# Third-layer attention units placed between second-layer units of later batches, in one fused four-layer kernel

## The chip, the cores and the metric

The kernel runs on one core of one Trainium2 chip. The metric is the time of one execution in device microseconds (us). Two differences matter for reading it: the time of an execution lies 1.7 us above the span that its profile covers, and the three timed executions before lie 0.15% apart.

## The reference

Four residual blocks run over x, four batches of 1024 tokens with 128 features, all float32. Each adds a layer-normed block output to x:

```
x = x + LN(attention0(LN(x)))     16 heads of 8, causal, scores clipped to +-10
x = x + LN(block1(LN(x)))         latent attention with rope, then a mixture of experts
x = x + LN(attention2(LN(x)))     16 heads of 8, causal, plain softmax
x = x + LN(low_rank_ffn(LN(x)))   128 -> 32 -> 512, gelu, 512 -> 32 -> 128
```

Batches are independent of each other. Within a batch each block needs the one before it. The latent attention has 16 heads; a head's query and key are 16 latent and 32 rope features wide, the key is the same for all heads. The experts are one shared and eight routed ones of which the two best count.

## The kernel before, in words

**Stages and units.** Three classes hold the work: `First` (attention0, L552), `Second` (block1, L675) and `Third` (attention2 and the low-rank part, L949). A stage is one class on one batch, 12 in all, numbered 0 to 11: 0 to 3 are First, 4 to 7 Second, 8 to 11 Third. A stage has four units of four heads, so there are 48 units. Before, units run in the order of their numbers: 0 to 15 First, 16 to 31 Second, 32 to 47 Third. A unit has 20 steps (`UNIT`), counted by `at`; step 20n is the start of unit n.

**The main loop** (L1341) runs over units, over two halves of 512 queries (`h`), and over tiles of keys. For each tile it records, on every engine's queue in program order:
- `scores` (L1251): TensorE multiplies keys by queries into PSUM tiles `ps_k`. Operands lie in `strips`, three buffers that units use in turn (`n % 3`). A First or Third head takes 32 rows of the TensorE array, so four heads can run side by side; a Second head takes 64 rows, so two can, and keys come from `kT`.
- `weigh` (L1265): ScalarE takes the exponential into `pt`; GpSimd masks the diagonal (L1279). For First, VectorE clips.
- `products` (L1213): TensorE multiplies `pt` by the values into `av`, a step or so later. At the end of a half ScalarE copies `av` to `num`, and `to_tokens` transposes and divides it.
- `max_step` (L1181): for Second and Third, whose softmax needs the row maximum, TensorE computes the scores of a *later* unit once more the other way round into `ps_q`, and VectorE reduces them to `mx`. `negated_rows` puts the negated maxima into a row of that unit's `strips`. `maxima` (L1328) sets the step at which each of a unit's 20 `max_step`s begins: 22 steps ahead for Second, 19 for Third, one a step.

In Third units `scores` takes one pair of heads (`pp`) at a time and the `max_step` beside it takes the other pair of the array's rows (L1359 to L1370); in First units `scores` takes both pairs at once.

**PSUM** has eight banks: in Second and Third one for `av` and a ring of seven (`ring`, L1344) for everything else, one bank of 512 columns a tile. A tile waits until the one seven tiles ahead of it has been read.

**Side work.** What stands before and after a stage's attention is cut into pieces by generators: `take_in` (norm, transposes, projections), `prepare` of each unit (fills its `strips` by DMAs; for Second also `roped`, L661: product, copy to `rb`, DMA that swaps neighbouring rows, two multiplications and an addition), and `tail` (output projection, norm, experts or low-rank part, residual). After each tile `other_work` (L1315) lets `pick` (L1285) choose pieces by due date: `ahead` (L1129) gives the steps before a unit's start in which `prepare` may begin and is due; inputs and tails have due dates at L1294 and L1249. What is not done when it is needed is finished on the spot, all its pieces one behind the other (`need_prep`, `need_input`, `need_tail`, `need_free`). A `prepare` of a unit that follows one of other layout clears its `strips` first (`clear`, L289: a memset and an addition on GpSimd).

**Queues.** The order of instructions on each engine is the program order; nothing is moved by a scheduler. DMAs go on SyncE's queue but for a few at the start.

**The last unit** (47) hands its rows in four quarters to `quarter` (L1045), which do the low-rank part of the last 1024 tokens, after what is left of the tails.

Of the kernel before, what the change touches and what calls it, by code (L numbers as in the profile page):

```python
# [16 lines left out]
P = 128  # L17
# [121 lines left out]
def sandwich(ctx: ExitStack, tc: tile.TileContext, a: dict, out: bass.AP):  # L139
# [69 lines left out]
    w3_n = stage[:, 2048 : 2048 + 3 * D]  # L209
# [5 lines left out]
    later(out=w3_n, in_=a["L1_attn_w_qkv"])  # L215
# [66 lines left out]
    w3 = ctile([P, 3, D], "w3")  # L282
# [23 lines left out]
    def prepare_weights():  # L306
# [74 lines left out]
        nc.gpsimd.tensor_copy(w3.rearrange("p s e -> p (s e)"), w3_n)  # L381

# [87 lines left out]
    def project(packed, w, xT, copy):  # L470

        yield RING, 1
        t = pool2.tile([P, T], F32, tag=f"packed{len(packed)}", name="packed")
        packed.append(t)
        by_half(copy, t, product(w, xT, "ps_p"))
# [76 lines left out]
    class First:  # L552
# [43 lines left out]
        def take_in(self):  # L596
            self.xT = new_xT("xT1")
            self.unit = {}
            if self.b == 0:
                xn = pool1.tile([P, NT, D], F32, tag="xn", name="xn")  # L600
                self.packed = [pool2.tile([P, T], F32, tag=f"packed{s}", name="packed") for s in range(2)]
                self.v, self.unit[0], self.mv = vs[0], strips[0], new_stats()
                yield from self.begin(xn, 0)
                self.second = Task(self.begin(xn, 1), 7)
                urgent.append(self.second)
                return
# [32 lines left out]
        def result(self, g, h):  # L639
            if g == 0 and h == 0:  # L640
                self.att = pool2.tile([P, NT, D], F32, tag="y", name="att1")
# [19 lines left out]
    def roped(dst, w, xT):  # L661
# [6 lines left out]
        nc.vector.tensor_tensor(dst[0:n], rb[0:n], cos[0:n], ALU.mult)  # L668
        for c in range(2):
            yield LIGHT, 2 * (1 - c)  # L670
            cols = slice(512 * c, 512 * c + 512)
            nc.gpsimd.tensor_tensor(swapped[0:n, cols], swapped[0:n, cols], sin[0:n, cols], ALU.mult)  # L672
            nc.gpsimd.tensor_tensor(dst[0:n, cols], dst[0:n, cols], swapped[0:n, cols], ALU.add)

    class Second:  # L675
# [41 lines left out]
        def prepare(self, g, n):  # L717
            if g == 0:
# [3 lines left out]
                self.kT = pool2.tile([P, T], F32, tag="packed0", name="kT2")  # L722
# [3 lines left out]
                rp = pool2.tile([P, T], F32, tag="packed1", name="rpk")  # L726
                yield from roped(rp, wkr.rearrange("p j r -> p (j r)"), self.xT)
                yield LIGHT, 2
                for j in range(2):
                    nc.sync.dma_start(out=self.kT[64 * j + 32 : 64 * j + 64], in_=rp[32 * j : 32 * j + 32])  # L730
            if g % 2 == 0:
# [4 lines left out]
                by_half(nc.scalar.copy, lat, product(w, self.xT, "ps_l"))  # L736
            yield RING, 1
            rp = pool2.tile([P, T], F32, tag="packed1", name="rp")
            yield from roped(rp, w2r[:, 4 * g : 4 * g + 4].rearrange("p h r -> p (h r)"), self.xT)
            yield LIGHT, 2  # L740
            while step_now[0] < strips_free(n):
                yield LIGHT, 1
            t = self.unit[g] = strips[n % 3]
            nc.sync.dma_start(
                out=t[R:P:64].rearrange("o s (q c) -> o (s q) c", q=NT),
                in_=no_max[0:2].unsqueeze(1).to_broadcast([2, 2 * NT, P]),
            )
            for j in range(4):
                pp, at, h = j // 2, 64 * (j % 2), 4 * (g % 2) + j
                nc.sync.dma_start(out=t[at : at + R, pp, :], in_=self.lat[R * h : R * h + R, :])  # L750
                nc.sync.dma_start(out=t[at + 32 : at + 64, pp, :], in_=rp[32 * j : 32 * j + 32, :])
# [197 lines left out]
    class Third:  # L949
# [8 lines left out]
        def take_in(self):  # L958
            self.unit = {}
            self.xT = new_xT("xT3")  # L960
# [7 lines left out]
        def prepare(self, g, n):  # L968
            yield LIGHT
            if n < 2 * B * NG + 3:  # L970
# [24 lines left out]
        def result(self, g, h):  # L995
            if g == 0 and h == 0:
                self.y = pool2.tile([P, NT, D], F32, tag="y", name="y3")
# [47 lines left out]
        def quarter(self, num, k):  # L1045
# [11 lines left out]
            if k == 1:  # L1057
                work, xb = tile("rb"), pool2.tile([P, T], F32, tag="packed0", name="xb")
# [70 lines left out]
    def ahead(u):  # L1129

        return (48, 44) if u.width == R else (40, 28) if u.has_max else (33, 8)
# [3 lines left out]
    units = [(layer[b], g) for layer in layers for b in range(B) for g in range(NG)]  # L1135
    stages = [u for layer in layers for u in layer]
    inputs = [Task(u.take_in(), u.pieces[0]) for u in stages]
    prep = [Task(u.prepare(g, n), (9, 4, 5, 4)[g] if u.width == R else 1) for n, (u, g) in enumerate(units)]
    tails = [None] * len(stages)
# [3 lines left out]

    def need_tail(k):

        while tails[k] is None or not tails[k].done:
            behind.popleft()[1].finish()

    def need_free(k):

        while not stages[k].att_free:
            behind[0][1].look(step_now[0])
            behind[0][1].piece(step_now[0])
            if behind[0][1].done:
                behind.popleft()

    def need_prep(n):
        for i in range(n + 1):
            if not prep[i].done:
                need_input(i // NG)  # L1160
                prep[i].finish()

    def need_input(k):
        for i in range(k + 1):
# [4 lines left out]

    def max_tiles(n):  # L1170

        mx, beside = {}, units[n][0].width != R
        for h in range(2):
            tiles = max_parts_of(h)
            if h and not beside:
                tiles = [tiles[i] for i in (0, 4, 1, 5, 2, 6, 3)]
            for i, parts in enumerate(tiles):
                for pp in (1, 0) if beside else (0, 1):
                    yield n, h, parts, pp, mx, i == len(tiles) - 1 and pp == 1 - beside

    def max_step(n, h, parts, pp, mx, last):  # L1181
# [4 lines left out]
        ps = rtile("ps_q")  # L1186
        for qt, c, at, w in parts:
            for jj in range(2):
                q, k = u.rows(g, pp, jj)
                nc.tensor.matmul(  # L1190
                    ps[jj][:, at : at + w], lhsT=q[:, qt * P : (qt + 1) * P], rhs=k[:, 512 * c : 512 * c + w],
                    start=True, stop=True,
                )
        for jj in range(2):
            for qt, c, at, w in parts:
                scores, to = ps[jj][:, at : at + w], mx[h][:, qt - 4 * h, pp, jj, c : c + 1]
                if c == h:

                    nc.vector.tensor_tensor_reduce(
                        scores, scores, cmask[:, 512 - w : 512], 1.0, -3.0e38, ALU.add, ALU.max, to  # L1200
                    )
                else:
                    nc.vector.tensor_reduce(to, scores, AX.X, ALU.max)
# [9 lines left out]
    def products(n, h, parts, first, last, state, pts):  # L1213
# [11 lines left out]
        if last:  # L1225
# [14 lines left out]
            k = n // NG  # L1240
            if g == 0 and h == 0 and k > 0:
                if u.width == R or stages[k - 1].width == R:
                    need_free(k - 1)
                elif k > 1:
                    need_free(k - 2)
            urgent.append(Task(back()))
            if g == NG - 1 and h == 1:
                tails[k] = Task(after(urgent[-1], u.tail()), u.pieces[1])
                behind.append((UNIT * NG * (k + 2) - 5, tails[k]))  # L1249
# [35 lines left out]
    def pick(at, taken):  # L1285
# [10 lines left out]
        if i is not None and inputs[i // NG].done and at >= UNIT * i - ahead(units[i][0])[0]:  # L1296
            found.append((UNIT * i - ahead(units[i][0])[1], prep[i]))
        k = next((k for k, t in enumerate(inputs) if not t.done), None)
        if k is not None and at >= UNIT * NG * (k - 1) and (k < B or tails[k - B] and tails[k - B].done):
            found.append((UNIT * NG * k - ahead(stages[k])[0], inputs[k]))  # L1300
        while behind and behind[0][1].done:
            behind.popleft()
# [24 lines left out]

    maxima = deque(  # L1328
# [101 lines left out]
```

## Time and profile before

| | |
|---|---|
| median of three executions | 2202.6 us (2199.86 to 2203.24) |
| profiled execution: time, span | 2196.13 us, 2194.4 us |
| TensorE matmul busy | 2062.8 us, 94% |
| VectorE busy | 1457.2 us, 66% |
| ScalarE busy | 1251.0 us, 57% |
| GpSimd busy | 589.5 us, 27% |
| mean granted TensorE clock | 0.97 |
| DMA | 20 GB/s, 42.93 MB |

The profile is of one execution. Busy TensorE time is the union of modelled matmul spans, and says nothing of how much of the array they fill: two heads on half of the rows count as much as four on all. Tiles go by the program's names; nearly all instructions have one line, L113, that of the recording helper. A unit's end is read from the trace as the start of the ScalarE copy `num<-av` of its second half.

### The profile page before, as it was taken

The page shows a single profiled execution, that of the slowest core. Times are in us where ns is not written, and L with a number is a line of the kernel's source. Part 1 is how long each engine was busy: PE and PEld are TensorE (multiplying, and loading weights), DVE is VectorE, ACT ScalarE, POOL GpSimd, SP SyncE. Part 2 cuts the span into 40 slices and gives each one's busy share as a digit, 9 for nine tenths or more (in the row PEclk, how much of TensorE's full clock was granted, in tenths as well). Part 3 has the DMA queues.
Part 4 walks back from the last instruction along what each step waited for, and adds up shares of the span by engine and source line. Part 5 has one row for each costly group of instructions (what it writes and reads, how often), then busy time and mean ns, then how long its engine had stood idle before and what let it go on. Part 6 is the DMA issues. An engine that isn't in the chain of part 4 may idle for free.

```text
span 2194.4 us, 40088 instructions
## 1 busy us (share of the span) xinstructions
PE 2062.8 (94%) x14480; PEld 939.4 (43%) x14480; DVE 1457.2 (66%) x4201; ACT 1251.0 (57%) x2360; POOL 589.5 (27%) x840
## 2 busy tenths in 40 slices
PE   7999999789999999999999999899999999999994
PEld 3334333334444544454444444344444444444432
DVE  4677776477666675567556675368778678777755
ACT  4777778524554554355534544255556766766775
POOL 3343333223232211222122311121113233323332
PEclk9999999989999999999999999899999999999996
DMA  2310000011111100111011100000000000000000
GB/s 59 69 17 11 12 11 11 21 38 25 28 42 26 25 16 22 35 29 26 6 30 35 29 13 1 11 7 7 6 7 7 12 7 16 8 11 17 7 1 20
DMA packets 32245, 42.93 MB, mean 20 GB/s; under 512 B 11552, under 2 KB 23840, under 8 KB 32048
## 3 DMA queue, kind: packets, MB, share of 16 engines
q1 hardware_dynamic: 31440, 40.04, 8.3%
q8 instruction: 115, 1.88, 0.3%
q14 instruction: 82, 0.67, 0.1%
q10 hardware_dynamic: 608, 0.33, 0.1%
HBM read 5.74 MB, written 2.10 MB: 4 GB/s over the span
## 4 chain that ended last, share of the span: by engine, by line
PE 82%; DVE 7%; ACT 5%; POOL 3%; issue 2%; DMA 1%; SPq 0%; ACTq 0%; POOLq 0%; DVEq 0%
PE ps_k L113 29%; PE ps_q L113 17%; PE av L113 17%; PE pgu L113 3%; ACT pt L113 2%; PE ps_a L113 2%; PE py L113 2%; DVE ps_q L113 2%; PE pa L113 2%; PE ps_p L113 1%; PE ps_o L113 1%; PE ps_t L113 1%; DVE mx L113 1%; DVE pt L113 1%; PE ps_l L113 1%
## 5 line engine op out<-in xcount | busy, mean ns | idle before, releaser
L113 ACT ACTIVATE pt<-ps_k 128x512 f32<-128x512 f32 (+2 forms) x1600 | 916.7, 631 | 621.4 <-PE ps_k L113 449.5
L1279 POOL TENSOR_SCALAR_AFFINE_SELECT pt<-pt 128x256 f32<-128x256 f32 (+1 forms) x576 | 302.8, 535 | 1209.4 <-ACT pt L113 887.4
L113 DVE CUSTOM_DVE_ANT_0 ps_q<-ps_q,cmask 128x512 f32<-128x512 f32 (+3 forms) x1024 | 488.4, 512 | 208.1 <-PE ps_q L113 187.6
L113 PE MATMUL ps_k<-strips 32*128 32x512 f32 (+3 forms) x3072 | 541.1, 527 | 9.8 <-DVE mx L113 4.9
L113 DVE TENSOR_REDUCE mx<-ps_q 128x1 f32<-128x512 f32 x512 | 328.3, 684 | 169.9 <-PE ps_q L113 168.5
L113 PE MATMUL ps_q<-strips 32*128 32x512 f32 (+3 forms) x1536 | 393.1, 530 | 14.1 <-DMA strips<-no_max 10.6
L113 PE MATMUL ps_q<-kT,strips 64*128 64x512 f32 (+3 forms) x1536 | 312.8, 491 | 25.1 <-DMA strips<-rp 24.2
L113 PE MATMUL av<-pt,vals 128*32 128x512 f32 (+3 forms) x3072 | 321.0, 500 | 15.7 <-POOL pt L1279 9.1
L113 PEld LDWEIGHTS ps_k<-strips 32*128 32x128 f32 x3072 | 220.2, 185 | 253.6 <-issue 76.3
L113 PE MATMUL ps_k<-strips,kT 64*128 64x512 f32 (+3 forms) x1536 | 323.3, 508 | 2.6 <-issue 2.6
L113 DVE TENSOR_SCALAR pt<-pt 128x1024 f32<-128x1024 f32 (+1 forms) x320 | 224.6, 717 | 115.7 <-ACT pt L113 114.1
L113 PEld LDWEIGHTS ps_q<-kT,strips 64*128 64x128 f32 x1536 | 150.0, 189 | 143.7 <-issue 100.5
L113 PEld LDWEIGHTS ps_k<-strips,kT 64*128 64x128 f32 x1536 | 133.9, 187 | 146.9 <-issue 66.2
L113 PEld LDWEIGHTS ps_q<-strips 32*128 32x128 f32 x1536 | 160.5, 184 | 64.8 <-ACT pt L113 26.2
L113 PEld LDWEIGHTS av<-pt,vals 128*32 128x32 f32 x3072 | 72.1, 109 | 218.6 <-issue 121.5
L113 PE MATMUL av<-pt,v2l 128*32 128x512 f32 (+3 forms) x1536 | 159.6, 503 | 0.0
L113 DVE DVE_READ_ACCUMULATOR2_ANT mx<- 128x1 f32 x1024 | 144.5, 141 | 0.0
L401 POOL TENSOR_TENSOR rs<-rs,minus_half 128x8 f32<-128x8 f32 (+1 forms) x38 | 63.6, 1674 | 242.4 <-DVE rs L113 239.6
L113 PEld LDWEIGHTS av<-pt,v2l 128*32 128x32 f32 x1536 | 33.7, 109 | 101.1 <-issue 72.7
L113 ACT COPY num<-av 128x512 f32<-128x512 f32 (+1 forms) x98 | 56.7, 581 | 19.8 <-PE av L113 19.7
L672 POOL TENSOR_TENSOR swapped<-swapped,sin 128x512 f32<-128x512 f32 (+1 forms) x40 | 50.8, 1271 | 63.1 <-DMA swapped<-rb 63.1
L113 PEld LDWEIGHTS ps_a<-ident,num 128*128 128x128 f32 x384 | 40.7, 141 | 61.7 <-issue 42.2
(278 smaller groups left out, 1646.0 us busy)
## 6 DMA issues: line engine op xcount, KB each, us to landing
swapped<-rb SPq DMA_DIRECT2D x32, 256.0 KB
strips<-rp SPq DMA_DIRECT2D x64, 128.0 KB
strips<-packed SPq DMA_DIRECT2D x248, 32.0 KB
strips<-lat SPq DMA_DIRECT2D x64, 64.0 KB
strips<-nT SPq DMA_DIRECT2D x256, 1.0 KB
strips<-nT SPq DMA_DIRECT2D x128, 2.0 KB
x<-in_L_attn_x_dram SPq DMA_DIRECT2D x3, 512.0 KB
out_dram<-x SPq DMA_DIRECT2D x3, 512.0 KB
```

What stands on the lines that cost most here:

```text
L113: return call(*args, **kw)
L401: nc.gpsimd.tensor_tensor(rs[:, t], rs[:, t], minus_half[:, t], ALU.pow)
L672: nc.gpsimd.tensor_tensor(swapped[0:n, cols], swapped[0:n, cols], sin[0:n, cols], ALU.mult)
L1279: nc.gpsimd.affine_select(out=corner, in_=corner, compare_op=ALU.is_ge, fill=0.0, base=0, pattern=[[0, 2], [0, n], [1, P]], channel_multip ...
```

## The change

The order of units is written out. Stages 0 to 5 run as before. Then units of stage 6 (Second, batch 2) alternate with those of stage 8 (Third, batch 0), and units of stage 7 with those of stage 9, with a last (7,2), (7,3), (9,2), (9,3). Stages 10 and 11 run as before. So units 24 to 39 mix both layers. What follows from it:
- The steps of `max_step` and `scores` change where neighbours differ. A Third unit behind a Second one (`together`) has its maxima of both pairs at once, four heads and four PSUM tiles in every second step. A Third unit before a Second one (`wide`) has its scores of both pairs at once. `beside`, one pair next to the other, stays between two Third units. The lead of the maxima is 19, 20 or 22 steps (`lead`).
- Due dates come from the new order (`due_input`, `due_tail`, `may_input`); tails that have not begun are sorted by due date. `ahead` is (40, 30) for Third, before (40, 28), and (34, 20) for First, before (33, 8).
- In Second units `other_work` is called twice a tile with a limit of three light pieces, before once with four.
- Buffers: `kT` has its own tag; `packed` and the results of First and Third (`yb`) have one buffer, before two; Second's result keeps two. With one buffer, a stage's first result waits for the tail of the stage before of the same layout (`need_free`). `roped` works in place in `rb`, and sends it by a function that it is given. `w3` takes the place of `w1` and is loaded by stage 8's `take_in`, without staging and copy.

```diff
-    w3 = ctile([P, 3, D], "w3")
+    w3 = w1
...
-    def roped(dst, w, xT):
+    def roped(w, xT, send):
         n = w.shape[1]
         rb = pool1.tile([P, T], F32, tag="rb", name="rb")
         by_half(nc.scalar.copy, rb[0:n], product(w, xT, "pa"))
         for o in range(2):
             nc.sync.dma_start(out=swapped[o:n:2, :], in_=rb[1 - o : n : 2, :])
-        nc.vector.tensor_tensor(dst[0:n], rb[0:n], cos[0:n], ALU.mult)
         for c in range(2):
             yield LIGHT, 2 * (1 - c)
             cols = slice(512 * c, 512 * c + 512)
+            nc.vector.tensor_tensor(rb[0:n, cols], rb[0:n, cols], cos[0:n, cols], ALU.mult)
             nc.gpsimd.tensor_tensor(swapped[0:n, cols], swapped[0:n, cols], sin[0:n, cols], ALU.mult)
-            nc.gpsimd.tensor_tensor(dst[0:n, cols], dst[0:n, cols], swapped[0:n, cols], ALU.add)
+            nc.gpsimd.tensor_tensor(rb[0:n, cols], rb[0:n, cols], swapped[0:n, cols], ALU.add)
+        yield LIGHT, 2
+        yield from send(rb)
...
-                self.kT = pool2.tile([P, T], F32, tag="packed0", name="kT2")
+                self.kT = pool2.tile([P, T], F32, tag="kT", name="kT2")
...
+            if self.b == 0:
+                yield LIGHT
+                nc.sync.dma_start(out=w3[:, 0:3], in_=a["L1_attn_w_qkv"].rearrange("p (s e) -> p s e", s=3))
...
-            if n < 2 * B * NG + 3:
+            if units[n - 3][0].width == R:
                 clear(strips[n % 3])
...
-                self.y = pool2.tile([P, NT, D], F32, tag="y", name="y3")
+                self.y = pool1.tile([P, NT, D], F32, tag="yb", name="y3")
...
-        return (48, 44) if u.width == R else (40, 28) if u.has_max else (33, 8)
+        return (48, 44) if u.width == R else (40, 30) if u.has_max else (34, 20)
...
-    units = [(layer[b], g) for layer in layers for b in range(B) for g in range(NG)]
+    whole = lambda *ks: [(k, g) for k in ks for g in range(NG)]
+    order = whole(0, 1, 2, 3, 4, 5)
+    order += [(6, 0), (8, 0), (6, 1), (8, 1), (6, 2), (8, 2), (6, 3), (8, 3)]
+    order += [(7, 0), (9, 0), (7, 1), (9, 1), (7, 2), (7, 3), (9, 2), (9, 3)] + whole(10, 11)
+    units = [(stages[k], g) for k, g in order]
...
+    def due_input(k):
+        return UNIT * starts[k] - (48 if stages[k].has_max else 34)
+
+    def due_tail(k):
+        return min([UNIT * (ends[k] + NG) - 5] + [due_input(k + B) - 28 if k < 2 * B else UNIT * len(units) - 30])
...
+    def beside(n):
+        return units[n][0].width != R and units[n - 1][0].width != R
+
+    def together(n):
+        return n < len(units) and units[n][0].width != R and units[n - 1][0].width == R
...
-        ps = rtile("ps_q")
+        tiles = [(pp, rtile("ps_q")) for pp in pps]
...
-            if g == 0 and h == 0 and k > 0:
-                if u.width == R or stages[k - 1].width == R:
-                    need_free(k - 1)
-                elif k > 1:
-                    need_free(k - 2)
+            if g == 0 and h == 0:
+                for m in like(k)[-1:]:
+                    need_free(m)
...
+    def lead(n):
+        return 19 if beside(n) else 22 if units[n - 1][0].width == R and not together(n) else 20
...
-        (UNIT * n + i - (22 if units[n][0].width == R else 19), m)
+        (UNIT * n + i * (1 + together(n)) - lead(n), m)
...
+                wide = not u.has_max or n == len(units) - 1 or u.width != R and units[n + 1][0].width == R
+                often = u.width == R or u.has_max and wide and n < len(units) - 1
+                pts = []
+                for pps in ((0, 1),) if wide else ((0,), (1,)):
+                    pts += [weigh(n, h, parts, ps) for ps in scores(n, h, parts, pps)]
+                    if not u.has_max:
+                        next_products(1)
+                    for pp in pps:
+                        at += 1
+                        if maxima and maxima[0][0] <= at:
+                            max_step(*maxima.popleft()[1])
+                        if pp == 0 and (u.has_max and (u.width != R or together(n + 1))):
+                            next_products(0)
+                        if pp == 0 and often:
+                            other_work(at, 3)
+                if u.has_max:
+                    next_products(0)
+                other_work(at, 3 if often else 4)
```

`like(k)` lists the stages of the same layout that run before stage k; `starts` and `ends` hold the unit at which a stage begins and the one after its last.

## The prediction

> **What bounds the kernel now.** First the page:
> ```profile
> span 2194.4 us, 40088 instructions
> PE 2062.8 (94%) x14480; PEld 939.4 (43%) x14480; DVE 1457.2 (66%) x4201; ACT 1251.0 (57%) x2360; POOL 589.5 (27%) x840
> ```
> TensorE (PE) looks full, but a matmul on half of the array's rows counts as one on all. So I cut the span at units (windows; the rows shown are units 14, 15, 16 to 23, 24 to 29, 30, and 36 to 46):
> ```profile
> core 0: us, PE busy (x) PEld busy (x) DVE busy (x) ACT busy (x) POOL busy (x), PEclk, DMA share, GB/s
> ...
> 401.80:465.70 63.90, 42.73 (x264) 16.80 (x264) 29.00 (x65) 24.04 (x34) 21.60 (x24) 0.84 0.15 39
> 465.70:522.70 57.00, 52.19 (x310) 20.90 (x310) 44.86 (x128) 22.30 (x34) 17.89 (x22) 0.94 0.15 35
> 522.70:962.60 439.90, 434.90 (x2738) 207.35 (x2740) 282.73 (x855) 220.60 (x450) 108.64 (x147) 0.99 0.10 26
> 962.60:1320.90 358.30, 350.68 (x2174) 170.05 (x2176) 232.22 (x700) 179.01 (x374) 82.16 (x112) 0.99 0.10 24
> 1320.90:1400.20 79.30, 68.65 (x384) 32.18 (x386) 33.47 (x85) 28.57 (x57) 13.43 (x17) 0.89 0.05 8
> ...
> 1649.70:2117.00 467.30, 462.45 (x3510) 208.30 (x3510) 351.82 (x1145) 317.19 (x672) 148.22 (x202) 1.00 0.05 10
> ```
> Then the timeline of PE, for what its work costs when nothing waits, a Second and a Third unit:
> ```profile
> 644.13 1.13 PE L113 MATMUL ps_k<-strips,kT 64*128 64x512 f32 x4
> 645.10 1.02 PE L113 MATMUL ps_q<-kT,strips 64*128 64x512 f32 x4
> 645.95 1.02 PE L113 MATMUL ps_k<-strips,kT 64*128 64x512 f32 x4
> ...
> 1800.30 0.70 PE L113 MATMUL ps_k<-strips 32*128 32x512 f32 x2
> ...
> 1800.84 0.59 PE L113 MATMUL ps_k<-strips 32*128 32x512 f32 x2
> ```
> Read starts, not durations. Two float32 matmuls of 512 columns on 64 rows each, two passes, take 645.95 - 645.10 = 0.85, so 0.43 us a pass; the one before came behind another array shape and took 0.97. Over the whole trace a pass that ends in a change of shape is 0.09 to 0.10 longer (`av` to `av` 0.453, `av` to 32 rows 0.543, median starts). With four groups of 32 rows a pass takes 0.53.
>
> From these I add up each unit's *dense* time: its passes at 0.43 per 512 columns of the full array, 0.095 a change of shape, 0.10 more for a 512 pass in four row groups. Measured less dense:
> - units 14 and 15 (First into Second): 120.9 - 72.0 = 48.9
> - 16 to 23 (Second): 439.9 - 414.2 = 25.7, 3.2 a unit; 24 to 29: 358.3 - 329.5 = 28.8, 4.8 a unit. 17 to 19, with little side work, lie at 0.5, 1.4 and 1.4.
> - 30 to 35 (Second into Third): 328.8 - 270.0 = 58.8
> - 36 to 46 (Third): 467.3 - 360.9 = 106.4, 9.7 a unit
>
> Second is bound by PE. Third is not: VectorE (DVE) is busy 351.8 of 467.3, 75%, against 64% in Second, and holds the banks:
> ```profile
> PEld ps_k L113 <- DVE mx L113: 41.9, 65, 1.0
> ```
> (waits, units 36 to 46). The two changes of layer hold stalls of their own, each with a cold clock behind it:
> ```profile
> PE ps_q L113 <- DMA strips<-rp: 18.7, 1, 18.7
> ...
> PE ps_q L113 <- DMA strips<-no_max: 10.6, 1, 10.6
> ```
> (waits of unit 14, then of unit 30). In 14, unit 16's whole `prepare` is finished on the spot, 419.9 to 445.9 on the chain. In 30, two strips are cleared at 1.81 + 1.89 each on GpSimd (POOL), then twelve DMAs go out, and clock 0.89 follows.
>
> **The change part by part.** Work on PE, DVE and ScalarE (ACT) stays the same: both programs hold the same matmuls and maxima. What differs is who stands beside whom. I took the dense time of each unit of the changed program from its order of instructions.
>
> *First into Second.* `ahead` of First lets unit 15's `prepare` go at step 266, due at 280 instead of 292; so unit 16's begins at step 284, not at 296, and is spread up to step 298; its first `max_step` comes at 300. The chain before, first product to landed strips, took 26.0; in place in `rb`, the second rope's copies wait for the first's DMA (2.3 by the chain's rows), so 29. Sixteen steps at 1.35 (27 a unit, units 12 and 13) cover 21.6; 7 remain where 18.7 stood. Unit 14 then has dense 28.9 + 6.5 (12 and 13: 7.1 and 6.0) + 7; unit 15 dense 39.3 + 13 (17.5 before, less 6% of 57 for the clock, and a little idling). Sum 94.7 against 120.9: 26 won. Bounds: 33 without the wait, 14 if 18.7 stays and only the cold clock goes.
>
> *Units 16 to 23.* Tail 4 is due at step 424, before 475, and squeezes into units 20 to 22. Dense 420.6, with 3.2 a unit 446.3: 6 lost.
>
> *The mixed units, 24 to 37.* Dense 659.6. A mixed pair has DVE work of a Second and a Third unit: (515.0 / 14 + 351.8 / 11) / 2 = 34.4 a unit, 66% of the 51.9 a unit that come out below. That is near Second's 64%, so I take the excess of units 24 to 29, 4.8, and not Third's 9.7: 659.6 + 14 x 4.8 = 726.8. Bounds: 1.1 (units 17 to 19) and 9.7. In its favour: four heads of one unit at once need no partner, while before `ps_k` and `ps_q` shared the array only if both had banks. Against it: `together` asks for four of seven banks at once.
>
> Inside this sum stands the price of the mixing: changes of array shape in units 24 to 46 go from 577 to 862 (32-row to `av`, which shows no price, left out). 285 x 0.095 = 27 us, already in the dense times.
>
> [...]
>
> *Units 38 to 46, Third alone.* Tail 7 now falls into units 38 to 40. Dense 329.3, with 9.7 a unit 416.6. Bounds: 7 a unit, since the fullest Third unit, 34 (dense 50.4), lay only 1.8 over; 11.7, if three runs of pieces finished on the spot (below) each stall 6.
>
> Units 24 to 46 together: 726.8 + 416.6 = 1143.4, before 358.3 + 79.3 + 249.5 + 467.3 = 1154.4: 11 won, the stall of unit 30 included. That stall goes since clears now come ten or more steps before use. There are eight clears instead of three, 5 x 3.7 = 18.5 more on POOL, which is 25% busy in these units. Cover: masks (`pt`) queue behind a clear and `av` behind them; `products` come a tile later, some 4 us, as long as a clear. If that cover fails, at most 18.5.
>
> *The end.* Before, twelve pieces of tail 10 are left after the loop; its last norm stands on the chain from 2139.94 to 2146.10. Now tail 10 ends in unit 47's first steps: 6 won.
>
> *At nothing:* `w3` is one DMA of 196 KB at step 450, used some steps later, with DMA at 10 to 26 GB/s; without that cover, a DMA wait like 10.6. The cosine product in halves adds some 0.15 x 20 on DVE, hidden as DVE has a third free. SyncE's DMAs are the same but for order; the maxima's `nT` queue behind strips that wait for a free `rb`, 20 steps ahead of use. Units 0 to 13: dense 302.1 to 303.4, 1 lost.
>
> Sum: 26 - 6 + 11 + 6 - 1 = 36. The profiled execution becomes 2196.1 - 36 = 2160; the median of the runs lies 6.5 above it, so 2202.6 - 36 = 2167.
>
> **Rivals.**
> 1. *Mixed units as dense as 17 to 19*, 1.1 a unit. For: the same DVE share, PE alone binding. Against: those units had hardly any side work. 14 x 3.7 = 52 more: 2115. Chance 0.17.
> 2. *Slower: the ring of seven banks.* In a `together` step four `ps_q` are read by DVE at 0.65 each, 2.6, and the next four can't start before; PE has `av`, `ps_k` and `ps_k` between, 1.0 + 0.95 + 0.86. On diagonal tiles (0.582 and 0.300 for two parts) DVE needs over 3. Then mixed units keep Third's 9.7: 14 x 4.9 = 69, and the median is 2202.6 + 33 = 2236. It decides from 4.8 + 36 / 14 = 7.4 a unit. Against: side work fills PE meanwhile, and half of the mixed units take two banks at a time. Chance 0.17.
> 3. *Work finished on the spot.* With one `yb`, units 33, 40 and 44 need the tail before at once: the instruction order shows 7 + 20, 29 + 20 and 7 + 20 pieces (of two tails) in one place. If each run idles PE like unit 30's stall, 10.6, then 30 are lost: 2197. For: unit 14 did this. Against: most pieces are norms on DVE and ACT, and experts' products follow each other with three in flight. Chance 0.10.
> 4. *The transition keeps its stall*, the change not doing what its due dates say: 26 less, 2193. Chance 0.06.
>
> **How the numbers follow.** The forecast has 0.50, its own range 2140 to 2195. Faster by over 0.2% (about what a measurement of this kernel can tell from no change): forecast, 1 and 4 and a part of 3, 0.77; within: 0.05; slower: rival 2 and a little, 0.18. The range from 2112 to 2214 leaves out half of rival 1 and most of rival 2.
>
> **What would show it.** Right: the first `ps_q` of unit 16 waits under 10 us and unit 14 takes under 50; no wait on `strips<-no_max`; units 27, 28, 30 and 35 (dense 37 to 40) end within 45; DVE busy near 66% in the mixed units; Third units from 41 on as before. Wrong: waits of `ps_q` or `ps_k` on `DVE mx` as long in the mixed units as in Third now (rival 2), or idle PE with a clock under 0.9 in units 33, 40 or 44 (rival 3).

## The result, and the profile after

The changed kernel takes 2270.8 us (median of four executions, 2269.0 to 2276.8) where the kernel before took 2202.0 beside it: a ratio of 1.0319, with a 95% interval of 1.0301 to 1.0336. It is slower by 3%, outside the forecast's range and above rival 2's 2236 as well. The profiled execution is a typical one, 2269.19 us with a span of 2267.5.

The page after, first its span and then the busy time of each engine:

```profile
span 2267.5 us, 40162 instructions
...
PE 2098.0 (93%) x14480; PEld 909.8 (40%) x14480; DVE 1483.1 (65%) x4221; ACT 1245.2 (55%) x2360; POOL 614.0 (27%) x849
```

The same 14480 matmuls are recorded as in the trace before. PE is busy 35 us longer, and idle 38 us longer (169.5 against 131.6). The windows of the changed kernel are cut at the same units as before: unit 14, unit 15, units 16 to 23, 24 to 37 (the mixed ones), 38 to 46, and the end.

```profile
core 0: us, PE busy (x) PEld busy (x) DVE busy (x) ACT busy (x) POOL busy (x), PEclk, DMA share, GB/s
413.10:462.30 49.20, 38.94 (x242) 13.81 (x242) 31.64 (x61) 23.68 (x33) 23.70 (x23) 0.90 0.19 51
462.30:521.50 59.20, 51.85 (x318) 20.44 (x316) 45.41 (x119) 21.99 (x33) 18.87 (x22) 0.94 0.09 23
521.50:978.10 456.60, 444.15 (x2742) 206.10 (x2742) 292.78 (x867) 221.77 (x459) 117.75 (x149) 0.99 0.10 25
978.10:1751.80 773.70, 733.48 (x4776) 305.76 (x4780) 492.93 (x1504) 388.00 (x818) 187.09 (x245) 0.97 0.07 17
1751.80:2195.20 443.40, 415.63 (x3065) 190.38 (x3062) 316.85 (x1003) 263.24 (x560) 113.87 (x160) 0.97 0.04 8
2195.20:2267.50 72.30, 42.96 (x279) 18.15 (x277) 33.31 (x118) 49.75 (x124) 16.07 (x25) 0.76 0.05 15
```

Read the first number behind the window, its length, against the prediction's terms:

| units | before | forecast | after | miss |
|---|---|---|---|---|
| 0 to 13 | 401.8 | 402.8 | 413.1 | +10.3 |
| 14, 15 | 120.9 | 94.7 | 108.5 | +13.8 |
| 16 to 23 | 439.9 | 446.3 | 456.6 | +10.3 |
| 24 to 46 | 1154.4 | 1143.4 | 1217.0 | +73.6 |
| the end | 77.4 | 71.4 | 72.3 | +0.9 |

Two thirds of the miss lie in units 24 to 46. DVE there is at 64% in the mixed units (492.93 of 773.7), a little under what the forecast took, so DVE did not become the bound. The waits of PE say what did happen:

```profile
PE av L113 <- POOL pt L1331: 32.3, 26, 6.7
PE ps_q L113 <- DVE mx L113: 23.9, 10, 10.7
PE ps_ct L113 <- DVE comb L113: 12.2, 3, 6.4
...
PE ps_q L113 <- DMA strips<-rb: 7.8, 1, 7.8
PE ps_k L113 <- DVE mx L113: 7.1, 7, 4.3
PE ps_o L113 <- ACT attT L113: 6.5, 2, 5.1
```

The columns are total us, number of waits, longest. The totals are made by a few long waits of *different* kinds: a mask on POOL (`pt`), the gates of the experts (`comb`), a norm (`mx`, 10.7, see below). The waits for strips are as forecast: one of 7.8 before unit 16's first `ps_q`, none on `no_max`.

Ten stalls of 2.5 us or more stand in units 24 to 46 (24, 25, 30, 32, 33, twice in 34, 39, 40 and 44); before there were three (26, 30 and 32). All but the one of 2.6 in unit 25 have a slow clock with them. Windows of the changed kernel right behind five of the stalls of the whole trace (the clock is the third number from the end):

```profile
785.00:800.00 15.00, 12.04 (x54) 5.42 (x56) 11.48 (x44) 3.82 (x9) 0.84 (x2) 0.77 0.00 0
...
1312.00:1325.00 13.00, 12.74 (x77) 5.18 (x81) 4.85 (x15) 4.26 (x11) 2.28 (x5) 0.77 0.27 58
1508.00:1522.00 14.00, 13.57 (x64) 4.88 (x64) 10.60 (x41) 7.08 (x17) 4.18 (x3) 0.72 0.00 1
...
1892.00:1910.00 18.00, 17.35 (x88) 5.68 (x88) 11.34 (x27) 11.55 (x25) 2.78 (x3) 0.83 0.11 17
2071.00:2085.00 14.00, 13.61 (x56) 4.68 (x56) 7.92 (x21) 8.93 (x21) 2.54 (x2) 0.71 0.19 36
```

**The account used from here on.** Each time of units 24 to 46 is split into four parts: the *dense* time of the prediction (with 0.095 a change of array shape in it), the time that PE is *idle*, the *clock* (half of PE's busy time in stretches where the clock records show 0.5; in these a pass of `ps_o`, 128x128, takes 0.213 before another, elsewhere 0.112, median starts in the changed trace), and the *rest*, which is what is left: what PE's work takes beyond dense at full clock, such as half-filled arrays (a pass of `ps_k` of 512 columns in two row groups of 32 takes 0.524 before `av`, in four 0.538, again in that trace). The *excess* over dense, by which the prediction goes, is idle, clock and rest together.

| kernel | units 24 to 46 | dense | shape changes | idle | clock | rest |
|---|---|---|---|---|---|---|
| before | 1154.4 | 960.3 | 577 | 28.1 | 14.4 | 151.6 |
| changed | 1217.0 | 988.9 | 862 | 68.0 | 25.8 | 134.3 |
| difference | +62.6 | +28.6 | +285 | +39.9 | +11.4 | -17.3 |

A part of the gain that the forecast counted on is there: the rest falls by 17.3. The shape changes are in the dense time as forecast, 27 us. The 51 us more of idle time and slow clock were not forecast.

### The profile page after: what moved, and what is told of

Same layout as the page of the kernel before. It is cut to its first block, busy times and chain, and to the rows that moved or that the text cites. A ratio compares the mean times of both kernels' runs of the same rounds, so it can differ in the third digit from the quotient of the medians.

```text
span 2267.5 us, 40162 instructions
## 1 busy us (share of the span) xinstructions
PE 2098.0 (93%) x14480; PEld 909.8 (40%) x14480; DVE 1483.1 (65%) x4221; ACT 1245.2 (55%) x2360; POOL 614.0 (27%) x849
## 4 chain that ended last, share of the span: by engine, by line
PE 77%; DVE 9%; ACT 5%; POOL 4%; issue 3%; DMA 1%; SPq 0%; ACTq 0%; DVEq 0%; POOLq 0%
PE ps_k L113 26%; PE av L113 17%; PE ps_q L113 17%; PE pgu L113 3%; PE ps_a L113 2%; ACT pt L113 2%; DVE ps_q L113 2%; DVE mx L113 2%; PE py L113 2%; PE pa L113 2%; PE ps_p L113 1%; PE ps_t L113 1%; PE ps_o L113 1%; PE ps_v L113 1%; DVE pt L113 1%
## 5 line engine op out<-in xcount | busy, mean ns | idle before, releaser
L113 PE MATMUL ps_k<-strips 32*128 32x512 f32 (+3 forms) x3072 | 476.1, 531 | 11.3 <-DVE mx L113 5.9
L113 PE MATMUL av<-pt,vals 128*32 128x512 f32 (+3 forms) x3072 | 338.1, 506 | 23.1 <-POOL pt L1331 17.8
L113 PE MATMUL ps_q<-kT,strips 64*128 64x512 f32 (+3 forms) x1536 | 335.8, 507 | 19.1 <-DVE mx L113 8.5
L113 PE MATMUL ps_k<-strips,kT 64*128 64x512 f32 (+3 forms) x1536 | 339.4, 523 | 4.7 <-issue 2.1
L113 PE MATMUL ps_q<-strips 32*128 32x512 f32 (+3 forms) x1536 | 302.7, 534 | 15.9 <-DVE mx L113 15.4
L113 PEld LDWEIGHTS ps_k<-strips 32*128 32x128 f32 x3072 | 193.6, 186 | 236.3 <-issue 94.2
L113 PEld LDWEIGHTS ps_k<-strips,kT 64*128 64x128 f32 x1536 | 133.1, 188 | 166.4 <-issue 64.5
L113 PE MATMUL av<-pt,v2l 128*32 128x512 f32 (+3 forms) x1536 | 167.6, 503 | 14.5 <-POOL pt L1331 14.5
L113 PEld LDWEIGHTS av<-pt,vals 128*32 128x32 f32 x3072 | 78.6, 109 | 234.7 <-issue 123.9
L113 PEld LDWEIGHTS ps_q<-strips 32*128 32x128 f32 x1536 | 121.5, 186 | 80.9 <-DVE mx L113 29.9
L113 PE MATMUL ps_a<-ident,num 128*128 128x128 f32 x384 | 65.5, 294 | 0.0
```

What stands on the lines that cost most here:

```text
L113: return call(*args, **kw)
```

## The experiments

**1. The changed kernel with the units in the old order.** Everything else of the change is kept: buffers, due dates, `roped` in place, `w3`.

```diff
-    order = whole(0, 1, 2, 3, 4, 5)
-    order += [(6, 0), (8, 0), (6, 1), (8, 1), ...
+    order = whole(0, 1, 2, 3, 4, 5, 6, 7, 8, 9, 10, 11)
```

> The changed kernel with its units in the old order (stages 0 to 11 one after the other), all else of the change kept. Theory A (the mixing leaves the tails too few units, so their chains and the runs of pieces finished on the spot stall PE): the stalls of units 20 to 40 of the changed kernel mostly go, those of the one result buffer (three runs) stay, the first transition's and the end's gain stay: 2195 to 2220 us. Theory B (buffers and due dates are what costs, whatever the order): 2245 us or more. Theory C (the mixed units themselves are slow, rival 2 of the forecast): below 2200, as nothing mixed is left.

Measured: 2212.4 us, ratio to before 1.006 (1.0041 to 1.0079), within theory A's range. So the mixing itself costs 58 us, and the rest of the change 12. Against this run, units 24 to 46 of the changed kernel are 53.6 longer: 21.9 by 231 more changes of shape, 32.6 idle, 6.4 clock, and -7.3 of all else. By region against before: units 0 to 13 +8.7, 14 and 15 -10.8, 16 to 23 +10.4, 24 to 46 +9.0, the end -3.4.

**2. Runs of pieces finished on the spot, in the kernel before.** `products` asks for the tail of the stage just before at the start of stages 9, 10 and 11, so that 14 pieces are finished at once in units 36, 40 and 44, as one `yb` would demand.

```diff
                 if u.width == R or stages[k - 1].width == R:
                     need_free(k - 1)
+                elif k > 2 * B:
+                    need_free(k - 1)
                 elif k > 1:
                     need_free(k - 2)
```

> The kernel before, in which a Third stage's first result needs the tail of the stage just before, not of the one before that; buffers as before. It makes three runs of 14 pieces (a whole norm and addition) finished on the spot, in units 36, 40 and 44, and nothing else. Theory A: each stalls PE for 4 to 5 us, as in unit 44 of the changed kernel, with a clock of 0.7 to 0.8 for some 14 us after: 7 to 9 each, so 21 to 27 in all, 2223 to 2229 us. If such runs lie beside other work (the forecast's view): under 5 more than before.

Measured: 2209.5 us, ratio 1.0045 (1.003 to 1.006), 9 more or 3 a run, between the two expectations. In its profiled execution, the slowest of its five, units 24 to 46 take 14.2 more, so 3 to 5 a run. PE idles 3.2 at each of the three places. A price, but not that of unit 30's stall.

**3. First's due dates alone, in the kernel before.**

```diff
-        return (48, 44) if u.width == R else (40, 28) if u.has_max else (33, 8)
+        return (48, 44) if u.width == R else (40, 28) if u.has_max else (34, 20)
```

> The kernel before with the lead of First's preparation (34, 20) instead of (33, 8), and nothing else. If the due date alone moves unit 16's preparation off the spot, units 14 and 15 lose 12 us as in the changed kernel (120.9 to 108.5), and units 0 to 13 stay at 401.8: 2190 us. If the 11 us that units 0 to 13 lost in the changed kernel come from this due date, nothing is left: 2200.

Measured: 2187.8 us, ratio 0.9947 (0.9931 to 0.9963), 12.7 won. Its waits, with two waits on `strips<-rp` besides the long one:

```profile
PE ps_q L113 <- DMA strips<-rp: 11.9, 3, 6.4
PE ps_q L113 <- DMA strips<-no_max: 10.6, 1, 10.6
```

The 18.7 became 6.4, and units 14 and 15 take 110.0. So the step works as described, but half of the 26 is all that it is worth. Units 0 to 13 take 407.4 here, 5.6 more than before.

**4. Gates: the transposes of `comb` later.** In the changed kernel TensorE's queue reaches `ps_ct` before DVE has ranked the experts (three waits, 12.2 together). The second number of a `yield` is the steps that must pass before the piece may be taken; here it is four instead of one.

```diff
-        yield (RING, 1)
+        yield (RING, 4)
         ps = rtile("ps_ct")
```

> The changed kernel in which the transposes of the expert gates come four steps, not one, after the piece that computes them on DVE. Theory A (PE waits for that chain with nothing put between): the waits of 6.4, 4.9 and 4.5 us before ps_ct in units 21, 32 and 39 go, with half as much for the clock: 2248 to 2258 us. If the waits only move to the next piece of the same tail: 2265 to 2275.

Measured: 2282.5 us, ratio 1.0377 (1.0361 to 1.0392), 12 *slower* than the changed kernel, and in neither expected range. Its waits no longer show `ps_ct` among the long ones, and show others:

```profile
PE ps_q L113 <- DVE mx L113: 34.5, 12, 10.7
...
PE ps_q L113 <- DMA strips<-rb: 10.1, 2, 6.2
```

The waits of units 21 and 39 at `ps_ct` went, but 3.1 in unit 21 and 3.0 in unit 39 came at `ps_q` and 3.8 in unit 22 (strips), and unit 33's wait at `ps_q` grew from 4.0 to 8.9. In unit 32, 3.6 of the 4.9 stayed: they are no wait of `ps_ct`, but of `ps_n`, the transposes of the negated maxima, which DVE makes behind the gates' ranking. A piece that is held back makes the pieces behind it late; the stalls moved.

**5 and 6. Tails without gates and experts, in both orders.** In both kernels `Second.tail` leaves out everything between the attention's residual and the last norm; 5 has the new order and 6 the old one.

```diff
-            mv = new_stats()
-            yield from stats(x2, mv)
...
             yield from add_normed(b, x2)
```

> The changed kernel with the gates and the experts left out of all four second-layer tails (the attention's output and the residual go straight to the last norm; the output is not the reference's). To be read against the next run, the same without the mixing. Theory A (the mixing costs only through tails that have too few units): with tails this short, mixed and unmixed lie within 10 us of each other, or mixed is faster by up to the 40 us that the forecast gave the fuller PE. Theory C (mixed units are slow in themselves): mixed is slower by 40 us or more, as with the tails (2270.8 against 2212.4).

> The changed kernel with its units in the old order and the gates and experts left out of the second-layer tails (the output is not the reference's). About 300 us less than with them, by the passes left out (53 us of PE work a stage and their share of stalls); what counts is its distance to the run before it: A 0 to 10 us below the mixed one or above it, C 40 us or more below it.

Measured: 2100.6 us for the new order (ratio to before 0.9551, 0.9537 to 0.9566) and 2059.9 for the old (0.9368, 0.9351 to 0.9384). Both are 150 to 170 us under the same kernel with gates and experts, where 300 was expected. With these gone from the tails, the mixing still costs 40.7 of the 58, just in theory C's range. Units 24 to 46 of the mixed kernel, then of the unmixed one:

```profile
930.30:2026.40 1096.10, 1050.18 (x7333) 438.44 (x7334) 726.16 (x2314) 620.65 (x1309) 296.30 (x401) 0.98 0.07 15
```

```profile
931.40:1985.90 1054.50, 1025.47 (x7337) 463.98 (x7338) 721.22 (x2315) 625.39 (x1318) 274.82 (x388) 0.99 0.07 14
```

PE is *busy* 24.7 longer (9.9 of it by the clock), at nearly the same number of matmuls (7333 and 7337 recorded), and idle 16.9 longer. By the account the 41.5 are +21.1 dense (251 more shape changes are 23.8 of it), +16.9 idle, +9.9 clock, -6.4 rest. So by the account about a half is the price of the shapes, which comes from the order of the matmuls themselves, whatever the tails do; so far theory C holds. The other half is stalls and slow clock, and the rest does not grow. The other 18 of the 58 need the gates and experts: without them the stalls of units 21, 32 and 39 are gone.

**7. The mask's wait.** In the changed kernel a Second unit before a Third one records its `products` in the middle of a step, where the mask of their `pt` may still be queued on POOL. Here they come at the end of the step, as in other Second units.

```diff
-                        if pp == 0 and (u.has_max and (u.width != R or together(n + 1))):
+                        if pp == 0 and u.has_max and u.width != R:
                             next_products(0)
```

The wait is unit 30's. POOL in the changed kernel, in order of time (start, duration, with what it waited for in brackets), and then PE:

```profile
1305.50 0.42 POOL L1331 TENSOR_SCALAR_AFFINE_SELECT pt<-pt 128x256 f32<-128x256 f32 x1 [5.72 <-ACT pt L113]
1305.90 1.70 POOL L668 TENSOR_TENSOR swapped<-swapped,sin 128x512 f32<-128x512 f32 x1
1307.67 1.60 POOL L669 TENSOR_TENSOR rb<-rb,swapped 128x512 f32<-128x512 f32 x1
1309.24 1.26 POOL L668 TENSOR_TENSOR swapped<-swapped,sin 128x512 f32<-128x512 f32 x1
1310.58 1.26 POOL L669 TENSOR_TENSOR rb<-rb,swapped 128x512 f32<-128x512 f32 x1
1311.79 1.01 POOL L1331 TENSOR_SCALAR_AFFINE_SELECT pt<-pt 128x256 f32<-128x256 f32 x2
```

```profile
1312.26 1.92 PE L113 MATMUL av<-pt,v2l 128*32 128x512 f32 x4 [3.19 <-POOL pt L1331]
```

Four rope operations run from 1305.90 to 1311.8, the mask behind them, and `av` behind the mask: POOL is a quarter busy and still holds PE for 3.19.

> The changed kernel with the products of a Second unit before a Third one at the end of each tile, as in other Second units, not in its middle. If the waits of av for the masks in units 30, 34 and 37 (3.2, 6.7, 2.8 and 1.8 us, the masks stand behind rope's work on GpSimd) come from that shorter distance, they go, with half as much for the clock: 2249 to 2258 us. If GpSimd is late by more than half a tile: 2265 to 2275.

Measured: 2252.0 us, ratio 1.0254 (1.0225 to 1.0282), 19 less than the changed kernel, within what was expected. The same wait in this kernel, where it was 32.3 with a longest of 6.7:

```profile
PE av L113 <- POOL pt L1331: 16.2, 21, 1.9
```

Units 24 to 46 take 1189.8, 27.2 less: idle -14.3, clock -10.5, and 100 shape changes fewer, -9.5 (the rest +7.1). Two thirds of the mixing's price remain.

**8. What is good in the change, without mixing.** The kernel before, with experiment 3's due dates, and the input of stage 8 due 30 steps earlier, so that strips are cleared before unit 30 needs them.

```diff
+        return (48, 44) if u.width == R else (40, 28) if u.has_max else (34, 20)
...
-            found.append((UNIT * NG * k - ahead(stages[k])[0], inputs[k]))
+            found.append((UNIT * NG * k - ahead(stages[k])[0] - (30 if k == 2 * B else 0), inputs[k]))
```

> The kernel before with the lead of First's preparation (34, 20), and the input of stage 8 due 30 steps earlier, so that the clearing of the first Third strips stands 20 steps ahead of their use; no mixing, buffers as before. The first wins 12.7 (measured), the second the 10.6 us of idle PE in unit 30 and some 6 for the clock behind it: 2169 to 2175 us. If the stall only moves to the next strips: 2185 to 2190.

Measured: 2176.9 us, ratio 0.99 (0.9872 to 0.9928), 2 above the expected range. It is 1% faster than the kernel before and 4% faster than the changed one. Unit 30 took 79.3 in the kernel before, 68.65 of them busy; here:

```profile
1313.20:1375.70 62.50, 62.50 (x363) 28.40 (x364) 37.55 (x91) 25.20 (x50) 9.75 (x15) 1.00 0.05 8
```

The unit is 16.8 shorter without the stall of 10.6 and the cold clock behind it; unit 29 ahead of it, to which pieces have moved, is 2.8 longer (60.6 against 57.8).

**9. Half the mixing.** Stage 7 alternates with stage 8, stage 6 runs before and stage 9 after them.

```diff
-    order = whole(0, 1, 2, 3, 4, 5)
-    order += [(6, 0), (8, 0), ...
+    order = whole(0, 1, 2, 3, 4, 5, 6)
+    order += [(7, 0), (8, 0), (7, 1), (8, 1), (7, 2), (8, 2), (7, 3), (8, 3)] + whole(9, 10, 11)
```

> Half of the mixing: stages 0 to 6 in the old order, then units of stage 7 (Second, batch 3) alternate with those of stage 8 (Third, batch 0), 8 mixed units in place of 16; the rest of the changed kernel is kept. The old order took 2212, the changed one 2271. Theory A (mixing has a price by the unit, in shape changes, stalls and the cold clock behind them): half of the 58, so 2235 to 2247, with some 120 to 160 shape changes more in units 24 to 46 than the old order's 631. Theory B (a single cause at one place, the tails of stages 6 and 7 crowded together among the mixed units 24 to 40): stage 6's tail has no Third unit beside it now, 2212 to 2225. Theory C (having only a few mixed units costs as much, as it is the changes between kinds that stall): 2260 or more.

Measured: 2245.6 us, ratio 1.02 (1.0175 to 1.0226): 33 of the 58, theory A's range. Shape changes are 741, 110 over the old order's 631, a little fewer than theory A's 120 and just under half of the way to 862. By the account, units 24 to 46 take 34.6 more than in the old order: +10.4 dense, +18.6 idle, +3.6 clock, +2.0 rest. The shapes go with the amount of mixing. The idle time, 18.6 of the full mixing's 32.6, does so in sum alone, since it stands in a few places: in unit 36 by itself PE waits 7.1 at `ps_ct` and 10.7 at a run of pieces.

**10. The longest stall, unit 40's.** The chain of the changed kernel up to it (start, duration, what):

```profile
1874.75 4.87 PE py L113 x40
...
1883.54 0.18 DVE rs L113
...
1883.80 1.65 POOL rs L397
...
1885.67 3.19 ACT ynorm L113 x8
...
1888.93 1.26 POOL x L430
1890.19 1.61 POOL rs L397
...
1891.83 0.17 DVE nb L113
1892.00 0.61 DVE mx L113
...
1892.65 2.67 PE ps_q L113 x4
```

This is a run finished on the spot: the last product of the experts, statistics, a root on POOL, norm on ACT, residual on POOL, the next root, and only then, in DVE's order, the `mx` that frees PE's bank. PE idles 10.7. With a buffer of its own for stage 10's result, neither unit 40 nor unit 44 needs these tails at once.

```diff
+                if self.b == 2:
+                    self.y = pool2.tile([P, T], F32, tag="kT", name="y3").rearrange("p (n d) -> p n d", n=NT)
...
-                for m in like(k)[-1:]:
+                for m in {10: [], 11: [9]}.get(k, like(k)[-1:]):
```

> The changed kernel, but stage 10's first result has a buffer of its own, so that units 40 and 44 need not finish tails 7, 9 and 10 on the spot; those pieces fall due later, part of them at the end. In the changed kernel unit 40 idled 10.7 us on TensorE and unit 44 4.2 at these places, with excesses of 20.3 and 20.9 where Third units had 9.7. Theory A (the run of pieces is the cause, cold clock included): 15 to 22 won, of which some 5 are given back at the end where tail 10 is left over again: 2253 to 2261. Theory B (the work of these tails costs the same wherever it stands, as three runs of 14 pieces made on the spot in the kernel before cost only 3 each): 2263 to 2271.

Measured: 2302.2 us, ratio 1.0456 (1.0424 to 1.0489), 31 slower than the changed kernel, and neither theory's range. Units 40, 42, 44 to 46 and the end of this kernel, and under it unit 40 and the end of the changed one:

```profile
1843.50:1894.50 51.00, 50.97 (x380) 22.96 (x374) 39.67 (x106) 24.67 (x51) 5.94 (x12) 1.00 0.07 11
1939.30:2003.80 64.50, 54.77 (x334) 24.97 (x334) 37.12 (x140) 32.28 (x71) 13.52 (x18) 0.87 0.03 5
2050.80:2179.40 128.60, 126.08 (x941) 55.96 (x945) 94.82 (x311) 77.87 (x166) 34.49 (x50) 0.98 0.05 10
2179.40:2293.40 114.00, 66.74 (x352) 28.70 (x344) 46.92 (x150) 71.31 (x165) 36.27 (x43) 0.71 0.03 8
```

```profile
1843.80:1921.90 78.10, 67.15 (x426) 31.80 (x423) 53.26 (x166) 31.57 (x70) 15.77 (x19) 0.91 0.03 5
...
2195.20:2264.50 69.30, 42.96 (x279) 18.15 (x277) 33.27 (x118) 49.75 (x124) 16.07 (x25) 0.77 0.04 12
```

Where the run stood, theory A holds: unit 40 has no idle PE and lasts 51.0 instead of 78.1, and units 44 to 46 take 15.7 less. But the pieces must stand somewhere. Units 41 to 43 are 27 longer (19 of it in unit 42, 64.5 against 45.4, with a stall of 5.8 on `strips<-no_max`), and the end, where no attention is left to hide them, 45 longer: 27.1 + 15.7 - 72 = -29, the span's difference. Of these two places the forced run is the cheaper one.

## Why the prediction was wrong

**The step that failed: the excess of a unit taken as an average.** The prediction gave every mixed unit 4.8 over its dense time and every Third unit 9.7. Measured less dense in the mixed units: units 25 to 29, 31, 35 and 36 have 5.8, 4.7, 5.3, 7.0, 3.7, 3.7, 4.9 and -0.5, together 34.6 where 38.4 were forecast. Units 24, 30, 32, 33, 34 and 37 have 11.6, 12.1, 10.5, 15.2, 18.2 and 11.8, 50.6 over the forecast. In the Third units, 39, 40, 44 and 46 are 30.1 over and the other five 3.3 under. So 4.8 was right for eight of the mixed units, with at most one stall of 2.6 among them, and ten units make 80.7, more than the whole miss of 73.6. That all mixed units are a little slower is not what the trace shows. Of the units that were to end within 45, 35 took 42.7 and 27, 28 and 30 took 45.1, 46.5 and 49.6.

The account says what the average hid. In the kernel before, the excess held few stalls: idle time and slow clock are 1.8 of the 4.8 a unit in units 24 to 29, and 0.4 of the 9.7 in units 36 to 46. In the changed kernel they are 4.0 a unit in the mixed units and 4.2 in units 38 to 46, while the rest is 4.1 and 8.5 a unit, near what was carried over (3.0 and 9.2). So some 64 of the 74 us are stalls and the slow clock with them, and the sum had no term for new ones.

**Why units stall.** In the kernel before, the side work beside a unit was mostly that of one layer. Mixed, tails 6 and 7, the `prepare`s with rope, the clears and the low-rank parts meet in the same units. The engines are not full: POOL is busy 24% and DVE 64% in units 24 to 37. What fails is the order: each engine does its queue in turn, and a mask behind four rope operations (unit 30; unit 34 behind squares of the gelu as well), transposes behind the gates' work on DVE (32 at `ps_n`, 39 at `ps_ct`), a maximum behind a norm (33, 40, 44) each hold PE for 3 to 11 us. Edits took single stalls away. With the products half a tile later (7) the long waits for masks went, and those of units 24 and 25 too, though unit 32's grew from 3.6 to 4.7. Without gates and experts (5) those of 32 and 39 went, and without the forced runs (10) those of 40 and 44. But of the changes of order only 7 gained on the whole: in 10, where tails fall due later, and in 4, where transposes and the tail behind them are held back, work and stalls moved to a worse place. Unit 33's stall is read from the trace alone. Why unit 24's (5.1, on `attT`) went in 7 stays open; it comes with the mixing, as experiments 5 and 9 have it (9 in its first mixed unit, 28) and the old order (1 and 6) has not.

**Its bounds.** The prediction did put a mask behind a clear on POOL, and took as cover that `products` come a tile, some 4 us, later. But a Second unit before a Third one records them in mid-step (experiment 7), and the four rope operations, 5.9 us in one piece with the mask behind, were not in its list. The bounds for the mixed units reached from 1.1 to 9.7 a unit, the averages of layers that run alone, and the measured mean of 114.0 / 14 = 8.1 lies within them. Units 38 to 46 have 12.7 a unit, above their upper bound of 11.7.

**First into Second** was mis-sized: 26 forecast, 12.4 measured. The wait is 7.8 (7 forecast). But the wait of 7.8 still has a cold clock with it, a stretch at 0.5 of 10.24; the sum for unit 14 had none. And unit 15 has a wait of 4.3 on `DVE mx`, as unit 16's first maxima now stand behind First's clipping on DVE, with a stretch of 6.83. Before, the stretches were 20.48, 3.41 and 3.41.

**Units 0 to 13** were to lose 1 and lost 11.3. A part is spread: the same instructions as before took 401.8 in its profile, in which the clock never fell there, and 405.1 in experiment 2. With First's new due dates they took 407.4 and 404.6 (experiments 3 and 8), and in the changed kernel and the seven experiments that keep its units 0 to 13 as they are 410.5 to 415.8. So the spread is some 3 to 5, the due dates' part, 2.5 between the means, lies within it, and the other 8 or so come with the rest of the change (the input's new rule, one `packed`), which was not taken apart.

**Units 16 to 23** were to lose 6 and lost 16.7. The squeezed tail 4 seems to cost more than its dense time: PE is idle 7.4 more in these units, 6.4 of it in unit 21 at `ps_ct`. Here too it is the order: on the chain to that wait, the gates' `rank`, `kept` and `comb` stand between maxima on DVE.

**What held.** The price of a change of shape: in the changed trace a pass of `ps_k` on 64 rows takes 0.429 before another of its kind and 0.526 before one on 32 rows (median starts), 0.097 more, a pair of shapes for which the prediction had no row. The end, 6 forecast and 5.1 measured. The stall on `no_max`, gone.

**The rivals.** Rival 2's sign came, though not its price. The row that the prediction read for Third, of weight loads that wait for `mx`, is there in the mixed units (waits, units 24 to 37):

```profile
PEld ps_q L113 <- DVE mx L113: 42.8, 49, 4.9
...
PEld ps_k L113 <- DVE mx L113: 11.3, 21, 1.0
```

That is 54.1 in 14 units, 3.9 a unit, where Third before had 41.9 and 4.0 of `ps_q` in 11 units, 4.2. PE itself idles only 7.8 for `mx` there. Over the whole trace it idles 31.0, and 23.3 of that are four waits in which a norm or a clip stands in front of the `mx`. What the banks cost beyond idle time can only stand in the rest: 4.1 a unit, where Second alone had 3.0 and Third 9.2. So the ring may have cost some 1.2 a unit, 16 us, and not the 4.9 of rival 2; no run took `together` back to settle it. That the mixed units' 8.1 lies above the 7.4 from which rival 2 decides is for another reason, the stalls.

Rival 3 named units 33, 40 and 44 and was right in that (4.0, 10.7, 4.2 idle; clock 0.72, 0.83, 0.71 behind); its 30 us are near what these units lost, 10.4 + 10.6 + 11.2 = 32 over the forecast's excess, but partly by luck, as it took 10.6 of idle time for each. Its chance of 0.10 was too low because it was taken as an alternative to the others, while it adds to them: stalls of several kinds, none of which decides alone.

## What to carry to other kernels

When work of two kinds is interleaved so that shares even out, don't give the new units the mean excess of the old ones, which holds the stalls of the old order: write down, for each engine, what will stand in front of the short operation that frees TensorE (a mask, a maximum, a transposed gate), since here it was this queue that stalled, with POOL at 24% and DVE at 64%, and not the share. Price a stall with the slow clock behind it (here 11.4 us beside 39.9 idle), and count array-shape changes before interleaving matmuls of different tilings; here they took some 27 us by the account. And when a piece is moved out of a bad place, ask where it goes: taken out of units 40 and 44 to 46, tails saved 43 us there and cost 72 elsewhere.

## What the runs showed of the hardware

In units 24 to 46 of both traces the slow clock comes in whole steps of 3.41 us. In the changed kernel's units 24 to 46 the clock records show eleven stretches, all at 0.5, of 3.41, 6.83, 10.24 or 13.65 us, one with every stall of 2.8 us or more, and two more in units 37 and 45, where no wait is longer than 1.8; they are 71.7 us, where before four made 37.6. The stalls of 3.2 (unit 30) and 2.8 us (unit 34) had 6.83 and 3.41 at 0.5 with them. A stall's length did not give the price: those of 4.5 (unit 39) and 4.2 us (unit 44) had 3.41 and 10.24 at 0.5.

A root of 128 x 8 elements on GpSimd takes 1.65 us (`rs`, median of 38), where DVE's step on `rs` ahead of it takes 0.18, and unit 40's run of pieces crosses it twice on its chain.
